# A new order of the first five attention units, and a last FFN group with the tokens on the partitions, both at once

## The chip, the cores and the metric

The kernel runs on one core of a Trainium2 chip. A core has five engines that run side by side, each taking its own instructions in order: TensorE (PE) multiplies matrices, VectorE (DVE), ScalarE (ACT) and GpSimd (POOL) work on elements, and SyncE (SP) here only issues DMAs. The metric is the device time of one execution in microseconds (us), the median over several executions.

## The reference

The program is one transformer layer in fp32: attention, then an FFN, each between two layer norms, with a residual added behind the second. x has 16 sequences of 256 tokens with 256 features.

```python
x = x + _layernorm(attn(_layernorm(x)))      # 16 heads of 128, causal softmax over 256 keys
x = x + _layernorm(ffn(_layernorm(x)))

# attn                                        # ffn; weights are 4-bit codes times a scale per block of 32
q = einsum('bpd,hde->bphe', x, W_Q) + b_Q     gate = einsum('th,nh->tn', xt, Wg)
k = einsum('bpd,hde->bphe', x, W_K) + b_K     up   = einsum('th,nh->tn', xt, Wu)
v = einsum('bpd,hde->bphe', x, W_V) + b_V     inter = gelu(gate) * up          # 2048 wide
z = softmax(causal(q k / sqrt(128))) v        out  = einsum('tn,hn->th', inter, Wd)
out = einsum('bqhe,hed->bqd', z, W_O) + b_O
```

## The kernel before

**Precision.** TensorE takes fp32r operands in one pass. To hold fp32 accuracy every large operand is split into a high half (the value rounded to fp32r, a copy on ACT) and a low half (the value less the high half, a subtraction on DVE or POOL), and a product is three matmuls, high by high, high by low, low by high (`mm3`). Small products (the own half of the scores, `qr` by `kr`) are true fp32 matmuls, which appear as two rows each. So each engine has its part in each operand: PE makes it, ACT the high half, DVE or POOL the low half.

**Attention.** The 4096 tokens are 8 blocks of 512 (two sequences). A unit is one head of one block, so there are 128 units; two heads make a pair, whose weights are split together. A unit passes these stages:

- `st_qk`: pk and pq, the keys and queries of 512 tokens, six matmuls of 512 columns each. ACT makes kh, kr, qh, qr; DVE makes kl, ql. pk and pq have one PSUM bank each, so the next unit's pk waits until ACT and DVE have read this one.
- `st_s`: scores of both sequences (sc), the mask and the row minimum on DVE (q carries a factor of -1/sqrt(128)), exp on ACT, the reciprocal rc on DVE, and the division pr on POOL.
- `st_t`, `st_w`, `st_b`: DVE transposes pr in 32x32 blocks (tr), four DMAs write it to HBM (hop) and one reads it back transposed (pt).
- `st_p`: high half of pt (ph) on ACT, low half (pl) on POOL.
- `st_v`: values of two pairs, one of four slices at a time (pv); `st_z`: z = v by probabilities (pz); `st_o`: the output projection, accumulated over the eight pairs (po).

The main loop runs over i from -5 to 129 and overlaps the stages: at step i it does the scores of unit i+4, q and k of unit i+5, pz of unit i, and between these it fills in other work by `slot`, which takes one piece from lists of pending jobs: weight splits (`splits`), layer norms (`urgent`, `behind`), the dequantization of FFN weights (`idle`). Of block 0 all raw weights come from HBM, are split and written back; later blocks load them already split. `w_split` is that split: high half on ACT, low half on POOL for v and o, on DVE for k and q.

**FFN.** It works on 1024 tokens at a time (superblocks of two blocks, bb = 0 and 1) in eight groups of 256 of the 2048 inner features, 32 groups in all. gate and up are made by a Strassen scheme with seven products in place of eight (m1 to m7), whose pieces ACT copies and DVE adds; gelu, the product and the halves of `inter` follow as a list of `pending` operations, of which one or two are issued beside each product. `st_d` multiplies the group before by wd and accumulates over the eight groups in four banks, pd (two blocks by two halves `dh` of the features). At a superblock's end `end` turns the sums so that the tokens lie on the partitions, and does layer norm and residual.

**The last group** has its own end, `st_last`: for four halves of 256 tokens (n = 0 to 3) it adds the last group's product, features on the partitions, to pd, copies it (oT on ACT), transposes it on PE (tpo, 16 transposes in all), takes mean and variance on DVE (one pow on POOL), and `apply` scales on DVE, shifts on ACT and sends it out: three outputs of 256 KB and two of 128 KB.

**Order.** Nothing is reordered by a scheduler: `run` (line 99 is where it calls every operation, so that all rows of the profile bear L99) ties each instruction behind the one issued before it on every engine, and `dma` (L88, L91) does that for SP. So the order in the source is the order on every engine, and an instruction that waits holds all behind it on its engine.

**The start.** While the first tokens are loaded, 30 transposes of the identity (`keep_warm`) run on PE; then `first_tokens` transposes the first normed tokens (tpx), and `w_split` makes the first weights.

Of the kernel before, what the change touches and what calls it, by code (L numbers as in the profile page):

```python
# [10 lines left out]
F32 = mybir.dt.float32  # L11
# [17 lines left out]
def kernel(  # L29
# [30 lines left out]
    def f(ap):  # L60
        return ap.bitcast(F32)
# [33 lines left out]
    def run(op, dst, *args, **kw):  # L95
        with ExitStack() as behind:
            for m in last.values():
                behind.enter_context(tc.issue_after(m))
            ins = op(dst, *args, **kw)  # L99
        last[ins.ins.engine] = ins.ins  # L100
        return ins
# [23 lines left out]
    def add(jobs, job, kind):  # L125
        jobs.append([job, 0, kind])
# [170 lines left out]
    def w_split(p, n):  # L297

        raw = RAW.pop((p, n)).rearrange("p (k c) -> p k c", k=2)
        key, done = p, True  # L300
        if n == "v":
            key, done = p // 2, p % 2
            w = HALF.pop(key) if done else w_tile(n)
            if not done:
                HALF[key] = w
            wv_ = w_view(w)[:, :, :, (p % 2) * 256 : (p % 2 + 1) * 256]
        else:
            w = w_tile(n)
            wv_ = w_view(w)
        c = qscale if n == "q" else 1.0  # L310
        run(nc.scalar.activation, wv_[:, 0], raw, AF.Copy, scale=c)
        if n in "vo" and (p, n) != (0, "v"):
            run(nc.gpsimd.tensor_tensor, wv_[:, 1], raw, f(wv_[:, 0]), ALU.subtract)
        else:
            run(nc.vector.scalar_tensor_tensor, wv_[:, 1], raw, c, f(wv_[:, 0]), ALU.mult, ALU.subtract)
        ahead = p + (2 if n == "v" else 1)
        if ahead < NG:
            w_raw(ahead, n)
        if done:
            W[key, n] = w_view(w)  # L320
            late.append((now[0] + 4, w_keep, (key, n, w)))
# [99 lines left out]
    def st_s(u):  # L421
        qh, ql, qr = Q.pop(u)
        kh, kl, kr = K.pop(u)
        pr = work.tile([P, 3, 2, P], F32, tag="pr", name="pr")
        mn = small.tile([P, 2, 2], F32, tag="mn", name="mn")
        sm = small.tile([P, 2, 2], F32, tag="sm", name="sm")
        rc = small.tile([P, 2, 2], F32, tag="rc", name="rc")
        parts = ((0, slice(0, 1)), (1, slice(1, 3)))
        scb = []
        for bi in range(2):  # L430
            sc = ps.tile([P, 3 * P], F32, tag="sc", name="sc", bufs=2)
            ks = slice(bi * S, (bi + 1) * S)
            run(nc.tensor.matmul, sc[:, 0:P], qr[:, bi, :], kr[:, bi, :], start=True, stop=True)
            mm3(sc[:, P:], [(lambda a: (qh, ql)[a][:, bi, :], lambda c: (kh, kl)[c][:, ks])])
            for q, cs in ((0, slice(0, P)), (1, slice(P, 3 * P))):
                run(
                    nc.vector.tensor_tensor_reduce,
                    sc[:, cs], sc[:, cs], mask[:, 2 * P - (cs.stop - cs.start) :], scale=1.0, scalar=3.0e38,
                    op0=ALU.add, op1=ALU.min, accum_out=mn[:, bi, q : q + 1],
                )  # L440
            scb.append(sc.rearrange("p (a c) -> p a c", a=3))
        while after:
            run(*after.popleft())
        for bi in range(2):
            for q, cs in parts:
                run(
                    nc.scalar.activation, pr[:, cs, bi, :], scb[bi][:, cs, :], AF.Exp,
                    bias=mn[:, bi, q : q + 1], scale=-1.0, accum_out=sm[:, bi, q : q + 1],
                )
            if bi:  # L450
                slot(V_, splits, idle, urgent, behind)
            run(nc.vector.reciprocal, rc[:, bi, :], sm[:, bi, :])
            for q, cs in parts:
                run(
                    nc.gpsimd.tensor_scalar, pr[:, cs, bi, :], pr[:, cs, bi, :], rc[:, bi, q : q + 1], 1.0,
                    ALU.mult, ALU.mult,
                )
        PR[u] = pr
# [22 lines left out]
    def st_p(u):  # L481
        pt = PT.pop(u).rearrange("p a m i -> p m a i")
        ph = work.tile([P, 2, 2, P], F32R, tag="ph", name="ph")
        pl = work.tile([P, 2, 2, P], F32R, tag="pl", name="pl")
        four = [t.rearrange("p c b (a i) -> p (c b) a i", a=4) for t in (ph, pl)]
        run(nc.scalar.copy, four[0], pt[:, 0:4])
        run(nc.gpsimd.tensor_tensor, four[1], pt[:, 0:4], f(four[0]), ALU.subtract)
        PH[u] = (ph, pl, pt)

    def st_z(u):  # L490
# [411 lines left out]
    def end(b, tr):  # L902
# [12 lines left out]
        for hf in range(2):  # L915
            dma(half(out, b, hf), X1[b][hf])

    def st_last():


        k = NGRP - 1
        while pending:
            run(*pending.popleft())
        w = FW[k, "d"]
        halves = [(bb, hf) for bb in (1, 0) for hf in range(2)]
        oTs, os, stats = {}, {}, {}

        def multiply(n, dh):
            bb, hf = halves[n]
            tok = slice(hf * S, (hf + 1) * S)  # L930
            cols = slice(dh * P, (dh + 1) * P)
            i = [quarter(k, c, bb) for c in range(2)]
            po = ACC[2 * NSB - 2 + bb, dh][:, tok]
            mm3(
                po, [(lambda a, c=c: w[:, a, c, cols], lambda s, c=c: i[c][:, s, tok]) for c in range(2)], MOVING_LAST,
                start=False, shared=True,
            )
            if dh == 0:
                oTs[n] = wide("oT").rearrange("p a b -> p (a b)")[:, 0 : 2 * S].rearrange("p (h n) -> p h n", h=2)
            run(nc.scalar.copy, oTs[n][:, dh], po)  # L940

        def turn_and_measure(n):
            tp = ps.tile([P, 2, D], F32, tag=("pk", "pq", "sc", "sc")[n], name="tpo", bufs=2 if n > 1 else 1)
            oT = oTs.pop(n)
            for t in range(2):
                for dh in range(2):
                    run(
                        nc.tensor.transpose,
                        tp[:, t, dh * P : (dh + 1) * P], oT[:, dh, t * P : (t + 1) * P], ident,
                    )  # L950
            os[n] = [tp[:, t, :] for t in range(2)]
            jobs = deque()
            stats[n] = None

            def measure():
                stats[n] = yield from ln_stats(os[n])

            add(jobs, measure(), V_)
            finish(jobs)

        def apply(n):
            bb, hf = halves[n]
            b = 2 * NSB - 2 + bb
            mv, rs = stats.pop(n)
            nb = ln_shift(mv, rs, 2)
            x1 = X1[b][hf]
            for t in range(2):
                run(
                    nc.vector.scalar_tensor_tensor,
                    x1[:, t, :], os[n][t], rs[:, t : t + 1], x1[:, t, :], ALU.mult, ALU.add,  # L970
                )
                run(nc.scalar.activation, x1[:, t, :], x1[:, t, :], AF.Identity, bias=nb[:, t : t + 1])
                if n == len(halves) - 1:
                    dma(half(out, b, hf)[:, t, :], x1[:, t, :])
            if n < len(halves) - 1:
                dma(half(out, b, hf), x1)

        count = len(halves)
        for n in range(count + 2):
            if n < count:  # L980
                multiply(n, 0)
            if 0 <= n - 1 < count:
                turn_and_measure(n - 1)
            if n < count:
                multiply(n, 1)
            if n >= 2:
                apply(n - 2)


    first = first_tokens()  # L990
# [13 lines left out]
        for n in range(count):  # L1004
            run(nc.tensor.transpose, warm[:, n % 4, :], ident, ident)

    keep_warm(30)
    add(urgent, first, V_)
    finish(urgent)
    run(nc.gpsimd.tensor_scalar, bqs, bqk[:, 0, :], qscale, 1.0, ALU.mult, ALU.mult)  # L1010
    for p in range(2):
        w_split(p, "v")
    for p, n in (2, "v"), (1, "k"), (1, "q"):
        w_get(p, n)

    def weights(*of):
        for pn, n in of:
# [3 lines left out]
    for i in range(-5, N + 2):  # L1021
        p = i // 2
        odd = i % 2 == 1
        if p >= 0 and not odd and p < len(pairs):
# [8 lines left out]
                    add(idle, f_make(*piece, pieces[m + 1] if m + 1 < len(pieces) else None), V_)  # L1033
            if b == NBLK - 1 and g == 0:
                add(spare, x_ops(0), N_)
        if 0 <= i + 4 < N:
            st_s(i + 4)
        slot(V_)
        if i + 5 < N:
            st_qk(i + 5)  # L1040
        slot(V_, urgent, behind)
        slot(G_)
# [19 lines left out]
            st_b(i + 3)  # L1062
        if 0 <= i + 4 < N:
            st_w(i + 4)
        if odd:
            weights((p + 1, "o"), (p + 5, "v"))
        else:
            weights((p + 4, "k"), (p + 4, "q"))
# [10 lines left out]
    for k in range(NGRP):  # L1079
# [18 lines left out]
        slot(V_)  # L1098
        slot(A_ + G_)
        st_d(k - 1, 1, 1)  # L1100
        slot(V_)
        slot(A_ + G_)
        if k > 0:
            parts(k, "m7", "m3")
        if k == NGRP - 1:
            parts(k, "m4")
        st_d(k - 1, 0, 0)
        slot(V_)
        slot(A_ + G_)
# [4 lines left out]
        slot(A_ + G_)  # L1114
    finish(urgent)
    finish(behind)
    st_last()


# [49 lines left out]
```

## Time and profile before

| | us |
|---|---|
| median of 3 runs | 1517.89 (1517.84 to 1518.86) |
| profiled execution | 1517.91, its span 1516.1 |
| PE busy | 1498.9 (99%) |
| DVE busy | 1185.8 (78%) |
| ACT busy | 1037.0 (68%) |
| POOL busy | 728.9 (48%) |
| first pk to first pz | 9.24 to 43.84 |
| last pe matmul, last tpo group, last output issued | 1496.87, 1508.61, 1513.2 |

Times inside the profile count from the start of the span; the execution's own time has 1.8 us more around it. The granted clock of TensorE is 0.998 over the span. A row of the timeline gives the start, the length, the engine, the operation and how many of them run together; in square brackets stands the idle time of the engine ahead of it and what ended that. Lengths of matmuls contain the way through the array, so the step from one start to the next is what one costs. The list of waits names what PE waited for: sum in us, how often, the longest.

### The profile page before, as it was taken

The page shows a single profiled execution, that of the slowest core. Times are in us where ns is not written, and L with a number is a line of the kernel's source. Part 1 is how long each engine was busy: PE and PEld are TensorE (multiplying, and loading weights), DVE is VectorE, ACT ScalarE, POOL GpSimd, SP SyncE. Part 2 cuts the span into 40 slices and gives each one's busy share as a digit, 9 for nine tenths or more (in the row PEclk, how much of TensorE's full clock was granted, in tenths as well). Part 3 has the DMA queues.
Part 4 walks back from the last instruction along what each step waited for, and adds up shares of the span by engine and source line. Part 5 has one row for each costly group of instructions (what it writes and reads, how often), then busy time and mean ns, then how long its engine had stood idle before and what let it go on. Part 6 is the DMA issues. An engine that isn't in the chain of part 4 may idle for free.

```text
span 1516.1 us, 25754 instructions
## 1 busy us (share of the span) xinstructions
PE 1498.9 (99%) x7831; PEld 1278.7 (84%) x7831; DVE 1185.8 (78%) x3011; ACT 1037.0 (68%) x2614; POOL 728.9 (48%) x951
## 2 busy tenths in 40 slices
PE   8999999999999999999999999999999999999997
PEld 7888888888888888888888888887888888888886
DVE  6876787787787888788778787777887887787866
ACT  6877766777677677676677767676766665666565
POOL 3755578677667776866876876880000000000000
PEclk9999999999999999999999999999999999999999
DMA  8998899999899999899899999977557465655561
GB/s 292 339 319 264 262 305 312 286 306 312 281 294 326 282 315 310 274 318 305 274 285 314 306 296 320 316 239 272 210 193 262 182 248 196 250 180 198 219 233 58
DMA packets 200426, 407.55 MB, mean 269 GB/s; under 512 B 21472, under 2 KB 128480, under 8 KB 189536
## 3 DMA queue, kind: packets, MB, share of 16 engines
q1 hardware_dynamic: 200288, 405.91, 79.9%
q8 instruction: 62, 1.02, 0.3%
q14 instruction: 76, 0.62, 0.1%
HBM read 294.15 MB, written 111.67 MB: 268 GB/s over the span
## 4 chain that ended last, share of the span: by engine, by line
PE 94%; DVE 2%; ACT 1%; DMA 1%; POOL 1%; issue 1%; SPq 0%; POOLq 0%; DVEq 0%; ACTq 0%
PE pd L99 13%; PE pk L99 11%; PE pv L99 11%; PE pq L99 11%; PE po L99 11%; PE pz L99 10%; PE sc L99 9%; PE pa L99 8%; PE pf L99 5%; PE pe L99 2%; DVE sum L99 1%; DMA rawq<-in_wq 0%; DMA rawv<-in_wv 0%; ACT pr L99 0%; DVE inter L99 0%
## 5 line engine op out<-in xcount | busy, mean ns | idle before, releaser
L99 POOL TENSOR_SCALAR pr<-pr,rc 128x128 f32<-128x128 f32 (+1 forms) x512 | 250.1, 504 | 90.7 <-DVE rc L99 90.7
L99 ACT ACTIVATE pr<-sc,mn 128x128 f32<-128x128 f32 (+1 forms) x512 | 208.2, 419 | 87.5 <-DVE mn L99 87.5
L99 POOL TENSOR_TENSOR rs<-rs,mhalf 128x4 f32<-128x4 f32 (+1 forms) x35 | 34.5, 985 | 485.1 <-DVE rs L99 275.0
L99 POOL TENSOR_TENSOR pl<-pt,ph 128x512 fp32r<-128x512 f32 x128 | 165.0, 1289 | 190.0 <-ACT ph L99 178.0
L99 DVE CUSTOM_DVE_ANT_0 sc<-sc,mask 128x128 f32<-128x128 f32 (+1 forms) x512 | 180.8, 374 | 67.8 <-PE sc L99 59.1
L99 PE MATMUL pv<-wv,xT 128*128 128x512 f32 x768 | 208.9, 407 | 0.0
L99 ACT ACTIVATE zh<-pz,bqk 128x512 fp32r<-128x512 f32 x128 | 88.3, 690 | 167.7 <-PE pz L99 167.6
L99 PE MATMUL pk<-xT,wk 128*128 128x512 f32 x768 | 199.5, 395 | 0.3 <-POOL xT L99 0.2
L99 PE MATMUL pd<-inter,wd 128*128 128x512 f32 (+1 forms) x792 | 197.8, 385 | 1.4 <-ACT inter L99 1.0
L99 PE MATMUL pq<-xT,wq 128*128 128x512 f32 x768 | 196.3, 391 | 0.0
L99 PEld LDWEIGHTS pd<-inter,wd 128*128 128x128 f32 x792 | 144.9, 188 | 34.5 <-DVE inter L99 2.9
L99 PEld LDWEIGHTS pq<-xT,wq 128*128 128x128 f32 x768 | 144.2, 188 | 32.9
L99 ACT COPY part<-pa 128x512 f32<-128x512 f32 x192 | 111.6, 585 | 68.0 <-PE pa L99 65.5
L99 PE MATMUL po<-zh,wo 128*128 128x512 f32 x512 | 157.7, 389 | 0.0
L99 PEld LDWEIGHTS pk<-xT,wk 128*128 128x128 f32 x768 | 134.9, 188 | 23.8 <-POOL xT L99 0.7
L99 PEld LDWEIGHTS pv<-wv,xT 128*128 128x128 f32 x768 | 135.0, 189 | 23.6
L99 DVE SCALAR_TENSOR_TENSOR zl<-pz,bqk,zh 128x512 fp32r<-128x512 f32 x128 | 95.9, 749 | 74.0 <-ACT zh L99 73.9
L99 ACT CAST inter<-sum 128x512 fp32r<-128x512 f32 x128 | 80.1, 626 | 87.5 <-DVE sum L99 87.5
L99 DVE TENSOR_TENSOR inter<-sum,inter 128x512 fp32r<-128x512 f32 x128 | 89.0, 695 | 56.9 <-ACT inter L99 55.9
L99 DVE STREAM_TRANSPOSE tr<-pr 128x768 f32<-128x768 f32 x128 | 123.3, 963 | 1.7 <-DMA hop<-tr 1.2
L99 DVE SCALAR_TENSOR_TENSOR kl<-pk,bqk,kh 128x512 fp32r<-128x512 f32 x128 | 96.1, 751 | 30.7 <-ACT kr L99 26.9
L99 PEld LDWEIGHTS po<-zh,wo 128*128 128x128 f32 x512 | 96.0, 188 | 19.9
(149 smaller groups left out, 3723.0 us busy)
## 6 DMA issues: line engine op xcount, KB each, us to landing
hop<-tr SPq DMA_DIRECT2D x512, 96.0 KB
pt<-hop SPq DMA_DIRECT2D x128, 384.0 KB
wk<-wk SPq DMA_DIRECT2D x64, 512.0 KB
wq<-wq SPq DMA_DIRECT2D x64, 512.0 KB
wo<-wo SPq DMA_DIRECT2D x64, 512.0 KB
wu<-fu SPq DMA_DIRECT2D x32, 1024.0 KB
wg<-fg SPq DMA_DIRECT2D x32, 1024.0 KB
wv<-wv SPq DMA_DIRECT2D x56, 512.0 KB
```

What stands on the lines that cost most here:

```text
L99: ins = op(dst, *args, **kw)
```

## The change

Five parts, made together:

1. `keep_warm` runs 27 transposes instead of 30.
2. In the first five steps (i < 0) `st_qk(i + 5)` is issued ahead of `st_s(i + 4)` instead of behind it, two slots for weight splits follow the scores, the slot for splits inside the softmax is left out for units below 4, and the split of v of pair 2 is asked for at i = -4 instead of ahead of the loop.
3. The low halves of the k and q weights of pairs 1 to 3 are made by POOL instead of DVE. For q, whose factor the DVE instruction applied on the way, POOL first multiplies the raw weights in place.
4. The low half of the probabilities, pl, of the last four units is made by DVE instead of POOL.
5. In the last group the sums of the first seven groups are copied by ACT (`copy_last`) and multiplied by the identity in true fp32 (`base_last`, eight matmuls of 128x128 for each block), which lays them with the tokens on the partitions into fresh banks; the last group's product is then made in that form too, with the tokens stationary and wd moving (48 matmuls of 256 columns as before), and added there. The 16 transposes and the eight copies oT of 256 columns fall away. `apply` scales and shifts on ACT for n < 3, and adds the residual on POOL, or, for the second tile of n = 0 and 1, on DVE after all multiplies were issued; the outputs are eight of 128 KB.

```diff
-        if n in "vo" and (p, n) != (0, "v"):
+        if n in "vo" and (p, n) != (0, "v") or n in "kq" and 1 <= p <= 3:
+            if n == "q":
+                run(nc.gpsimd.tensor_scalar, raw, raw, c, 1.0, ALU.mult, ALU.mult)
             run(nc.gpsimd.tensor_tensor, wv_[:, 1], raw, f(wv_[:, 0]), ALU.subtract)
...
-            if bi:
+            if bi and u >= 4:
                 slot(V_, splits, idle, urgent, behind)
...
-        run(nc.gpsimd.tensor_tensor, four[1], pt[:, 0:4], f(four[0]), ALU.subtract)
+        engine = nc.vector if u >= N - 4 else nc.gpsimd
+        run(engine.tensor_tensor, four[1], pt[:, 0:4], f(four[0]), ALU.subtract)
...
+    def copy_last(bb):
+        OT[bb] = wide("oT").rearrange("p a b -> p (a b)").rearrange("p (h n) -> p h n", h=2)
+        for dh in range(2):
+            run(nc.scalar.copy, OT[bb][:, dh], ACC.pop((LAST[bb], dh)))
+
+    def base_last(bb):
+        oT = OT.pop(bb)
+        for hf in range(2):
+            to = BASE[bb, hf] = ps.tile([P, 2, D], F32, tag=(("po0", "po1"), ("pv", "pz"))[bb][hf], name="base")
+            for t in range(2):
+                for dh in range(2):
+                    run(
+                        nc.tensor.matmul, to[:, t, dh * P : (dh + 1) * P],
+                        oT[:, dh, (2 * hf + t) * P : (2 * hf + t + 1) * P], ident,
+                        start=t == 0 and dh == 0, stop=False, skip_group_check=True,
+                    )
...
+        def multiply(n):
             bb, hf = halves[n]
             i = [quarter(k, c, bb) for c in range(2)]
             for t in range(2):
+                tok = slice((2 * hf + t) * P, (2 * hf + t + 1) * P)
+                mm3(
+                    BASE[bb, hf][:, t, :],
+                    [(lambda s, c=c: i[c][:, s, tok], lambda a, c=c: w[:, a, c, :]) for c in range(2)],
+                    start=False, shared=True,
+                )
...
+            if n < 3:
+                fa = wide("fa")
+                for t in range(2):
+                    ln_apply_act(fa[:, t, :], o[t], nb, rs, t)
+                    where = nc.vector if t and n < 2 else nc.gpsimd
+                    todo = (where.tensor_tensor, x1[:, t, :], x1[:, t, :], fa[:, t, :], ALU.add)
+                    if where is nc.vector:
+                        rest.append((todo, to[:, t, :], x1[:, t, :]))
+                    else:
+                        run(*todo)
+                        dma(to[:, t, :], x1[:, t, :])
...
+        for n in range(4):
+            multiply(n)
+            if n == 1:
+                base_last(0)
+            measure(n)
+            if n:
+                apply(n - 1)
+        for todo, to, x1 in rest:
+            run(*todo)
+            dma(to, x1)
+        apply(3)
...
-    keep_warm(30)
+    keep_warm(27)
...
-    for p, n in (2, "v"), (1, "k"), (1, "q"):
-        w_get(p, n)
+    for n in "kq":
+        w_get(1, n)
...
+        if i < 0:
+            while after:
+                run(*after.popleft())
+            st_qk(i + 5)
         if 0 <= i + 4 < N:
             st_s(i + 4)
+        if i < 0:
+            for _ in range(2):
+                slot(V_, splits)
         slot(V_)
-        if i + 5 < N:
+        if 5 <= i + 5 < N:
             st_qk(i + 5)
...
+        if i == -4:
+            w_get(2, "v")
...
         st_d(k - 1, 1, 1)
+        if k == NGRP - 1:
+            copy_last(1)
...
             parts(k, "m4")
+            base_last(1)
         st_d(k - 1, 0, 0)
...
     finish(behind)
+    copy_last(0)
     st_last()
```

More of the change, by code (lines that the diff above doesn't have):

```diff
@@ L916, in end @@
             dma(half(out, b, hf), X1[b][hf])
+    OT = {}
+    BASE = {}
+    LAST = [2 * NSB - 2, 2 * NSB - 1]
+    def copy_last(bb):
[13 more added lines that the diff above has]
+                    )
     def st_last():
@@ L925, in st_last, with measure, work_ @@
         halves = [(bb, hf) for bb in (1, 0) for hf in range(2)]
-        oTs, os, stats = {}, {}, {}
-        def multiply(n, dh):
+        stats, sums = {}, {}
+        rest = []
+        def multiply(n):
             bb, hf = halves[n]
-            tok = slice(hf * S, (hf + 1) * S)
-            cols = slice(dh * P, (dh + 1) * P)
             i = [quarter(k, c, bb) for c in range(2)]
[L933 to L944, printed above, removed]
-            for t in range(2):
[L946 to L951, printed above, removed]
-            jobs = deque()
[L953 to L958, printed above, removed]
+            for t in range(2):
+                tok = slice((2 * hf + t) * P, (2 * hf + t + 1) * P)
[4 more added lines that the diff above has]
+                )
+        def measure(n):
+            jobs = deque()
+            o = [BASE[halves[n]][:, t, :] for t in range(2)]
+            def work_():
+                mv, rs = yield from ln_stats(o)
+                stats[n] = o, mv, rs
+            add(jobs, work_(), V_)
             finish(jobs)
@@ L962, in apply @@
             bb, hf = halves[n]
-            b = 2 * NSB - 2 + bb
-            mv, rs = stats.pop(n)
+            o, mv, rs = stats.pop(n)
             nb = ln_shift(mv, rs, 2)
[L966 to L987, printed above, removed]
+            x1 = X1[LAST[bb]][hf]
+            to = half(out, LAST[bb], hf)
+            if n < 3:
[9 more added lines that the diff above has]
+                        dma(to[:, t, :], x1[:, t, :])
+            else:
+                for t in range(2):
+                    run(
+                        nc.vector.scalar_tensor_tensor,
+                        x1[:, t, :], o[t], rs[:, t : t + 1], x1[:, t, :], ALU.mult, ALU.add,
+                    )
+                    run(nc.scalar.activation, x1[:, t, :], x1[:, t, :], AF.Identity, bias=nb[:, t : t + 1])
+                    dma(to[:, t, :], x1[:, t, :])
+        for n in range(4):
[9 more added lines that the diff above has]
+        apply(3)
     first = first_tokens()
```

## The prediction

> **What bounds the kernel now.** I read the page's busy shares first, then the list of all waits of PE, then three stretches of the timeline: the start, the seam between attention and FFN, and the tail.
>
> ```profile
> PE 1498.9 (99%) x7831; PEld 1278.7 (84%) x7831; DVE 1185.8 (78%) x3011; ACT 1037.0 (68%) x2614; POOL 728.9 (48%) x951
> ```
> PE works 99% of the span, so the change can save or lose only where PE waits, or where it adds or removes PE work, or behind PE's last matmul.
>
> ```profile
> PE sc L99 <- ACT qr L99: 5.1, 4, 2.0
> PE warm L99 <- POOL ident masks.py:199: 1.6, 1, 1.6
> PE pd L99 <- ACT inter L99: 1.0, 3, 0.4
> PE pz L99 <- POOL pl L99: 0.9, 1, 0.9
> ...
> PE tpo L99 <- ACT oT L99: 0.3, 1, 0.3
> ```
> These are PE's waits (sum in us, times, longest). Nearly all of the 5.1 us lies in the first five units; the `pl` wait is one, at the seam.
>
> ```profile
> 9.24 1.62 PE L99 MATMUL pk<-xT,wk 128*128 128x512 f32 x6
> ...
> 20.81 0.49 PE L99 MATMUL sc<-kr,qr 128*128 128x128 f32 x2 [1.96 <-ACT qr L99]
> ...
> 43.84 0.28 PE L99 MATMUL pz<-ph,vh 128*128 128x256 f32 x1
> ```
> From the first matmul to the first pz: 34.6 us. By the same timeline pk+pq take 2.73 (41.12 to 43.84), a unit's scores 1.32 (20.81 to 22.13), a pv 1.40: 6x2.73 + 5x1.32 + 4x1.40 = 28.6, so 6.0 us are stalls.
>
> ```profile
> 36.52 0.83 POOL L99 TENSOR_SCALAR pr<-pr,rc 128x128 f32<-128x128 f32 x2 [3.84 <-DVE rc L99]
> 38.52 1.11 POOL L99 TENSOR_SCALAR pr<-pr,rc 128x128 f32<-128x128 f32 x2 [1.17 <-DVE rc L99]
> 40.33 1.29 POOL L99 TENSOR_TENSOR pl<-pt,ph 128x512 fp32r<-128x512 f32 x1 [0.70 <-DMA hop<-tr]
> 41.58 1.29 POOL L99 TENSOR_TENSOR wo<-rawo,wo 128x512 fp32r<-128x512 f32 x1
> 43.21 1.62 POOL L99 TENSOR_SCALAR pr<-pr,rc 128x128 f32<-128x128 f32 x4 [0.34 <-DVE rc L99]
> ```
> POOL before pz(0): `pl` is finished at 41.6, 2.5 us before PE uses it at 44.07, and nothing but pr stands ahead of it.
>
> ```profile
> 1499.46 0.62 ACT L99 CAST inter<-sum 128x512 fp32r<-128x512 f32 x1 [1.43 <-DVE sum L99]
> 1500.86 2.51 PE L99 MATMUL pd<-inter,wd 128*128 128x256 f32 x16 [0.22 <-DVE inter L99]
> ...
> 1503.20 0.60 PE L99 MATMUL tpo<-ident,oT 128*128 128x128 f32 x4
> ...
> 1508.32 5.28 SPq L91 DMA_DIRECT2D out<-xs  x5
> ```
> The tail: the cast of the last group's `inter` opens the final multiplies; the last of five output DMAs is issued at 1513.2.
>
> **The change part by part.** The sum is made against the profiled execution: 1517.91 us, span 1516.1 and 1.8 around it; that is the median of 1517.89. For start and tail I walked each engine's new order forward, every instruction starting when its engine is free and its inputs done, with the durations of before's rows.
>
> *Start, fewer warm transposes and the new order.* Three warm transposes less at 0.11 (3 in 7.58 to 7.91): -0.3, because the token transposes (7.15) follow the last warm one directly. In the new order PE has pk/pq(1) in front of sc(0), and pv+pk/pq in front of each later score, so qr has more cover. The stalls left in the walk: 0.7 at pk(1) (its bank is free only after kr(0) on ACT), 0.9 at one pv, 2.2 before sc(4), where only pv lies between sc(3) and it; together 3.9 instead of 6.0. First pz at 41.6 instead of 43.84: **-2.3**. The lo halves of pairs 1 and 2 on POOL fall into its idle time (3.84 before 36.52); the moved (2,v) fetch and the earlier weight DMAs on SP shift no operand that PE waits for, since the raws land before their splits. If they did not, a k/q DMA would show as a wait of ACT for wk, priced among the rivals.
>
> *Start, lo halves of k,q of pair 3 on POOL.* They are issued ahead of `pl` of unit 0. In the walk POOL ends pr(3) at 39.3 and then runs wk lo 1.25, raw*c, wq lo 1.26, pl 1.25. The price of raw*c (one 128x512 tensor_scalar) is not in the trace. Near rows: pr, the same operation with one scalar, 0.48 for 128 and 0.52 for 256 columns on average, alone 0.83 for the two; xn with two pointer scalars 1.23 for 256 columns. Bounds 0.52 and 2x1.23=2.46; I take 0.70, since pr is the same kind and 0.83 buys 384 columns with two starts. pl is then done at 43.8, while PE wants it at 41.8: a **new stall of 2.0**. Queued behind it on POOL are wo lo (1.29) and pr(4) (1.63), which ends at 46.7 instead of 44.8; pr(4) holds tr (0.97), zl (0.75) and the masks of unit 5 on DVE, these hold exp(5) on ACT, and that the copies up to qr(6): sc(6) waits 1.2 instead of 0.1, **+1.1**. Net of the start -2.3+2.0+1.1 = **+0.8**; each us more of raw*c goes on 1:1, so from +0.6 to +3.0 (the walk with 2.46 gave +3.5, because the next unit slips too).
>
> The Trainium skill speaks against this move: "GPSIMD Engine Reference", section "Engine selection", sends elementwise work to the Vector engine because two-input operations take about twice as long on GpSimd. The rows agree in size (1.29 against 0.69), but the rule by itself would price it at 4x0.6=2.4, while here the queue makes it 3.1. The page's "Elementwise" section has 768 ns for a one-input loop of 512 elements; with that estimate for raw*c the start would be +0.9.
>
> *Seam.* `pl` of the last four units goes from POOL (1.29) to DVE (0.69).
>
> ```profile
> 1006.62 2.45 POOL L99 TENSOR_SCALAR xn<-xs,mv,rs 128x256 f32<-128x256 f32 x2
> 1009.04 1.26 POOL L99 TENSOR_TENSOR pl<-pt,ph 128x512 fp32r<-128x512 f32 x1
> ...
> 1010.36 0.39 PE L99 MATMUL pz<-pl,vh 128*128 128x256 f32 x1 [0.88 <-POOL pl L99]
> ```
> POOL has xn ahead of pl; DVE is busy 4.3 of the 8 us from 1004 to 1012, so it does pl well before 1009.5: **-0.9**. Bounds 0 and -0.9.
>
> *Tail.* T is the start of the last pe matmul (1496.87). Before pd's twelve matmuls there now stand eight fp32 matmuls of base_last(1). Their price: from 44.19 (pt,vr, the same fp32 128x128) to 44.54 lie one such and one 256-column matmul, 0.35-0.12=0.23; 8 of them 1.8. Nothing covers them, PE being the bound there. pd ends at T+4.7 instead of T+2.9. ACT runs in order, and copy_last(0) puts two copies of pd ahead of the waiting cast: the second starts when pd is done, 0.48 later the cast starts, at T+5.4 instead of T+2.6 (1499.46). Cast to the first final multiply and lo half on DVE as before: the multiplies flow from T+6.8 instead of T+4.0: **+2.8**. From there before ran 48 multiplies, 16 transposes and 2 waits to 1509.43 = T+12.6; now 46x0.118 and the second base_last 1.8 end at T+14.2, so **PE ends 1.65 later**, the transposes (16x0.09) and their waits being gone.
>
> The Trainium skill's "FP8 and Floating Point Precision", "TensorE Precision Notes", gives true FP32 four passes: 4x128 columns cost what 512 do, 1.8 for eight by the 0.23 of such a step. The rows of tpo (0.36 for four, 1503.20 to 1503.56), to which a multiplication by the identity looks alike, would give 0.7 a base_last, and the tail 1.8 to 2.2 less.
>
> copy_last(1) costs ACT two copies of 0.48 in the last group, where it had 1.91 idle ahead of the cast at 1496.88; I cost it at nothing (without that cover 1.0).
>
> Behind PE: statistics, pow and POOL's two adds for n=2, then SP, which now issues eight outputs of 128 KB instead of five, takes n=2's two, the two deferred ones and the last two, in that order. An add of 256 columns on POOL lies between 0.46 (128 columns, 64 rows `full<-full`) and 1.29 (512); I take 0.73, in proportion. In the walk n=2's second output is issued at T+17.7 and four more issues follow 0.39 and 3x0.48 apart: the last at T+19.55, instead of T+16.29 (1513.16). The landing (1.9 before) stays. Tail **+3.3**; with the adds at their bounds +2.8 to +5.0, contention of the deferred DVE adds with POOL up to +0.4.
>
> Sum: +0.8 - 0.9 + 3.3 = +3.2, with a little for that contention: 1517.9+3.3 = **1521.2**.
>
> **The rivals.**
> 1. *The start keeps its gain.* If POOL is through pair 3's halves before about 40.5 (2 us earlier than in the walk), pz(0) does not wait and pr(4) is not late: 1517.9-2.3-0.9+3.3 = 1518.0. For it: POOL's gap of 3.84 before 36.52. Against: its queue is in order, and pr(3) waits for exp(3), which sits ahead of the halves.
> 2. *POOL is dearer.* raw*c at 2.46 and the tail's adds at 1.29: +2.7+1.7 on 1521.2 = 1525.6; one of them alone 1523 to 1524. For it: xn's 1.23. Against: pr's 0.52.
> 3. *Faster.* The start loses all its stalls, 6.0+0.3, and no new one comes: 1517.9-6.3-0.9+3.3 = 1514.0. It decides if ACT, DVE and POOL each keep under PE's 5.45 a unit (2.73+1.32+1.40) with nothing queued between exp and the next qr. Against: DVE alone is busy 25.2 of the 35 us from 9 to 44, and masks, exp, pr, tr stand in one chain.
> 4. *The identity is cheap.* base_last as the transposes: 1519.2.
>
> **How the numbers follow.** A measurement of this kernel tells about 0.2% (3.0 us) from no change: 1514.9 and 1520.9. Chances: forecast 0.52 (its own range 1520.3 to 1522.6, longer upwards by the contention), rival 1 0.16, rival 2 0.19, rival 3 0.06, rival 4 0.07. Slower is rival 2 and three quarters of the forecast: 0.58; faster rival 3: 0.06; within: 0.36. The range leaves out rival 3, the lower part of rival 1 and the upper half of rival 2: 1518.2 to 1523.9.
>
> **What would show it.** Start: the first pz about 2 us earlier, PE waiting for `pl` there and for qr at sc(6). Seam: no pz wait for POOL. Tail: two oT copies ahead of the `inter` cast on ACT, base matmuls 0.22 apart, the last output issued 19.5 after the last pe matmul. It is wrong if pz(0) finds pl ready, if raw*c takes over 1 us, or if base matmuls step by 0.11.

## The result, and the profile after

The changed kernel takes 1522.89 us (median of eight), the kernel before 1518.94 in the same comparison: 3.95 us more, a ratio of 1.0024 with a 95% interval from 1.0016 to 1.0033. The prediction was 1521.2 from 1517.9, that is +3.3, in a range of 1518.2 to 1523.9. The direction, the size and the places were right. Of the three terms of the sum, the seam was off by 0.3 us, the tail by 0.6 and the start, by execution, by 0.1 to 1.1, and one thing happened that no step had named. Of the 1.7 us by which the time itself was missed, 1.0 is the base: the kernel before took 1517.89 in the runs that the prediction started from and 1518.94 here.

The profiled execution has a span of 1521.4. The busy line of its page:

```profile
PE 1502.3 (99%) x7844; PEld 1282.0 (84%) x7844; DVE 1183.0 (78%) x3005; ACT 1038.1 (68%) x2610; POOL 736.3 (48%) x960
```

PE has 3.4 us more busy time; part of it is the slower clock shown below. The list of PE's waits of the changed kernel (sum in us, how often, the longest):

```profile
PE sc L99 <- ACT pr L99: 2.1, 1, 2.1
...
PE base L99 <- ACT inter L99: 1.2, 1, 1.2
PE pv L99 <- DVE vl L99: 1.1, 2, 0.8
...
PE sc L99 <- ACT qr L99: 0.8, 1, 0.8
PE pk L99 <- DVE kl L99: 0.6, 1, 0.6
PE pz L99 <- POOL pl L99: 0.6, 1, 0.6
```

The 5.1 us of waits for qr are down to 0.8, and four other waits have taken their place: for exp ahead of sc(4) (2.1), for vl, for kl, and for pl at the first pz. The wait of 0.9 at the seam is gone. Its rows in the timeline, DVE starting pl 1.1 us before PE takes it:

```profile
1009.92 0.75 DVE L99 TENSOR_TENSOR pl<-pt,ph 128x512 fp32r<-128x512 f32 x1
...
1011.03 0.28 PE L99 MATMUL pz<-pl,vh 128*128 128x256 f32 x1
```

The start, PE's rows of the timeline of the changed kernel:

```profile
9.53 1.60 PE L99 MATMUL pk<-xT,wk 128*128 128x512 f32 x6
...
38.19 0.80 PE L99 MATMUL sc<-kr,qr 128*128 128x128 f32 x2 [2.15 <-ACT pr L99]
...
43.74 0.28 PE L99 MATMUL pz<-ph,vh 128*128 128x256 f32 x1
...
44.69 0.39 PE L99 MATMUL pz<-pl,vh 128*128 128x256 f32 x1 [0.55 <-POOL pl L99]
...
59.92 0.28 PE L99 MATMUL pz<-ph,vh 128*128 128x256 f32 x1
```

The first pz comes at 43.74 as before (43.84), not at 41.6, and the third, from which on up to the seam every unit takes the same time in both kernels, 1.7 later (58.21 before). The queue on POOL that the prediction had named is there, row for row, about 0.8 later than in its walk:

```profile
38.43 1.63 POOL L99 TENSOR_SCALAR pr<-pr,rc 128x128 f32<-128x128 f32 x4 [4.13 <-DVE rc L99]
40.02 1.29 POOL L99 TENSOR_TENSOR wk<-rawk,wk 128x512 fp32r<-128x512 f32 x1
41.40 0.62 POOL L99 TENSOR_SCALAR rawq<-rawq 128x512 f32<-128x512 f32 x1
42.10 1.29 POOL L99 TENSOR_TENSOR wq<-rawq,wq 128x512 fp32r<-128x512 f32 x1
43.36 1.28 POOL L99 TENSOR_TENSOR pl<-pt,ph 128x512 fp32r<-128x512 f32 x1
```

But PE came late to it, because of something else. In the windows of the changed kernel (stretch, length, busy time and instructions of PE, PEld, DVE, ACT and POOL, granted clock, DMA share, GB/s) the granted clock falls to half for 3.4 us, right behind the wait ahead of sc(4):

```profile
34.80:38.20 3.40, 1.25 (x7) 0.69 (x5) 3.06 (x12) 1.51 (x7) 0.00 (x0) 1.00 1.01 313
38.20:41.60 3.40, 3.40 (x13) 3.21 (x14) 1.77 (x6) 3.30 (x9) 3.08 (x6) 0.50 0.98 374
41.60:45.00 3.40, 2.85 (x14) 2.25 (x14) 1.68 (x9) 3.07 (x12) 3.32 (x4) 1.00 0.98 335
```

The tail, rows of the timeline of the changed kernel:

```profile
1498.61 1.95 PE L99 MATMUL base<-ident,oT 128*128 128x128 f32 x16
...
1503.34 0.59 ACT L99 COPY oT<-pd 128x512 f32<-128x512 f32 x1 [0.77 <-PE pd L99]
1503.82 0.62 ACT L99 CAST inter<-sum 128x512 fp32r<-128x512 f32 x1
...
1505.22 2.90 PE L99 MATMUL base<-wd,inter 128*128 128x256 f32 x22 [0.22 <-DVE inter L99]
...
1510.94 8.04 SPq L91 DMA_DIRECT2D out<-xs  x8
```

Counted from the start of the last pe matmul (T, here 1498.38), the cast stands at T+5.4 and the flow of multiplies at T+6.8, both as predicted. PE ends at T+14.4 (14.2 predicted) and the last output is issued at T+20.20 (19.55 predicted, 16.29 before).

### The profile page after: what moved, and what is told of

Same layout as the page of the kernel before. It is cut to its first block, busy times and chain, and to the rows that moved or that the text cites. A ratio compares the mean times of both kernels' runs of the same rounds, so it can differ in the third digit from the quotient of the medians.

```text
span 1521.4 us, 25795 instructions
## 1 busy us (share of the span) xinstructions
PE 1502.3 (99%) x7844; PEld 1282.0 (84%) x7844; DVE 1183.0 (78%) x3005; ACT 1038.1 (68%) x2610; POOL 736.3 (48%) x960
## 4 chain that ended last, share of the span: by engine, by line
PE 93%; DVE 2%; ACT 2%; POOL 1%; issue 1%; DMA 1%; SPq 0%; POOLq 0%; DVEq 0%; ACTq 0%
PE pd L99 13%; PE pk L99 11%; PE pv L99 11%; PE pq L99 11%; PE po L99 11%; PE pz L99 9%; PE sc L99 9%; PE pa L99 8%; PE pf L99 5%; PE pe L99 3%; DVE sum L99 1%; PE base L99 1%; DMA wu<-fu 1%; PE warm L99 0%; ACT pr L99 0%
## 5 line engine op out<-in xcount | busy, mean ns | idle before, releaser
L99 POOL TENSOR_TENSOR pl<-pt,ph 128x512 fp32r<-128x512 f32 x124 | 160.0, 1291 | 184.8 <-ACT ph L99 175.4
L99 PE MATMUL pd<-inter,wd 128*128 128x512 f32 x744 | 190.7, 391 | 1.0 <-ACT inter L99 1.0
L99 PEld LDWEIGHTS pd<-inter,wd 128*128 128x128 f32 x744 | 138.8, 188 | 33.2 <-DVE inter L99 2.4
L99 PEld LDWEIGHTS pv<-wv,xT 128*128 128x128 f32 x768 | 134.7, 189 | 24.9 <-DVE vl L99 1.5
```

## The experiments

Two ways to explain the start stood against each other: F, POOL's queue ahead of pl, as predicted; and C, the half clock. For the tail: ACT's order and the outputs behind PE (F, O), or the fp32 matmuls themselves (B). All of them compute the whole layer.

The times of e1 to e6 and e9 against before have intervals of some 1.4 us to either side, and e7 and e8 were timed in one execution each, so single profiles, read row by row, carry most of what follows. The table has the eleven profiles, in us from the start of the span; "clock up" is where the steps of the first matmuls fall from 0.21 to 0.11, "half clock" a stretch at half the granted clock between 10 us and the end of PE's work.

| kernel | clock up | first pk | first pz | third pz | third pz less first pk | half clock | T to last output issued |
|---|---|---|---|---|---|---|---|
| before | 6.3 | 9.24 | 43.84 | 58.21 | 48.97 | - | 16.29 |
| e2 (start as before) | 4.4 | 8.67 | 43.74 | 58.14 | 49.47 | 21.4-24.9 | 20.18 |
| e9 (start as before) | 5.9 | 8.77 | 43.91 | 58.28 | 49.51 | - | 16.30 |
| changed | 7.5 | 9.53 | 43.74 | 59.92 | 50.39 | 38.2-41.6 | 20.20 |
| e1 | 7.6 | 9.61 | 43.91 | 60.01 | 50.40 | 38.3-41.7 | 16.29 |
| e3 | 5.9 | 8.74 | 41.64 | 59.08 | 50.34 | - | 18.24 |
| e7 | 5.9 | 9.06 | 42.00 | 59.43 | 50.37 | - | 16.27 |
| e5 | 7.0 | 9.28 | 42.18 | 60.15 | 50.87 | 44.5-47.9 | 16.91 |
| e4 | 5.7 | 8.90 | 41.81 | 58.52 | 49.62 | - | 20.21 |
| e6 | 5.4 | 8.74 | 41.69 | 58.39 | 49.65 | - | 16.28 |
| e8 | 5.7 | 8.73 | 39.76 | 59.06 | 50.33 | 1050.1-1053.5 | 16.29 |

### e1: all but the last group

The changed kernel with `st_last` of before, and without the calls

```diff
-            copy_last(1)
...
-            base_last(1)
...
-    copy_last(0)
```

> The change without its part 5: the last group as before, with 16 transposes. Theory F, the forecast: start +0.8, seam -0.9, so -0.1 us against before (within 1 us), and all of the loss of the whole change is in the last group. Rival C: the start alone already costs 1.5 us or more, because TensorE runs at half its clock for three microseconds after the wait ahead of sc(4) (granted clock 0.50 from 38.2 to 41.5 in the profile of the changed kernel): +1 to +2 against before. If the slow stretch is an accident of one execution, this profile shows none and PE waits about 2 us for pl at the first pz.

Measured: ratio 1.0008 (0.9999 to 1.0017), +1.2 us; the forecast's -0.1 is just inside. The half clock appears again, at the same place, and the third pz is 1.8 later than in before, so up to here C stands as well as F. T to the last output is 16.29, to the hundredth as in before: whatever the new tail costs is in part 5 alone.

### e2: the last group alone

The kernel before with `st_last` of the changed kernel, and the calls

```diff
+            copy_last(1)
...
+            base_last(1)
...
+    copy_last(0)
```

> Before with part 5 alone. Theory F: +3.3 us, with the last pe matmul where it was, the last multiply 1.6 later and the last output issued 3.3 to 3.8 later relative to the last pe matmul. Rival: the new tail is worth nothing by itself and the loss of the whole change comes from the start: within 1 us of before.

Measured: 1.0028 (1.0019 to 1.0037), +4.2 us, T to the last output 20.18. So the tail is worth +3.9 by the profiles, and the rival is out. This profile had a surprise: the start of before loses its clock too, as its windows show, behind its own longest wait, the one ahead of sc(1):

```profile
18.00:21.40 3.40, 1.15 (x8) 0.84 (x7) 2.94 (x6) 2.98 (x7) 1.48 (x3) 1.00 0.68 192
21.40:24.80 3.40, 3.40 (x13) 2.81 (x12) 2.60 (x11) 2.08 (x9) 0.63 (x2) 0.51 0.92 267
```

### e3: the cast ahead of the copies

In the changed kernel:

```diff
         while pending:
             run(*pending.popleft())
+        copy_last(0)
...
     finish(behind)
-    copy_last(0)
     st_last()
```

> The changed kernel, with the copies of the first block's sums (copy_last(0)) issued behind the pending operations of the last group instead of ahead of them. Theory F (ACT's order holds the cast): the cast starts 2.6 instead of 5.4 after the last pe matmul, multiplies 2.0 earlier (they then wait for pd, which the eight fp32 matmuls still delay), the end 1.8 earlier than the changed kernel, about +2 against before. Rival B (the 16 fp32 matmuls of 0.22 are what costs, wherever the cast stands): no more than 0.5 earlier than the changed kernel.

Measured: 1.0021 (1.0012 to 1.0030), +3.2 us; its profile holds 2.0 us of waits for a weight DMA (wu) in the FFN, which the changed kernel's list does not have, so the rows decide. Tail of e3, with T at 1499.71:

```profile
1502.29 0.62 ACT L99 CAST inter<-sum 128x512 fp32r<-128x512 f32 x1 [1.43 <-DVE sum L99]
...
1504.46 3.04 PE L99 MATMUL base<-wd,inter 128*128 128x256 f32 x24
...
1510.31 8.04 SPq L91 DMA_DIRECT2D out<-xs  x8
```

The cast is at T+2.6, the multiplies flow from T+4.75, PE ends at T+12.45, where before ended at T+12.56, and the last output is issued at T+18.24: **1.96 of the tail's 3.9 us were ACT's order**. And rival B falls: with ACT's order mended, the 16 fp32 matmuls (0.22 each in the steps of PE's rows, two rows of 0.11) cost no more than the transposes, oT copies and waits that they replace.

This execution kept its clock, and there the start is the predicted one: first pz at 41.64, and

```profile
43.86 0.39 PE L99 MATMUL pz<-pl,vh 128*128 128x256 f32 x1 [1.82 <-POOL pl L99]
```

a wait of 1.8 for pl (2.0 predicted), the third pz 0.87 later than in before (0.8 predicted). That this is so close is in part luck: the first pk came at 8.74 here, 0.2 ahead of the 8.94 that the prediction had.

### e4: pair 3 on DVE

In the changed kernel:

```diff
-        if n in "vo" and (p, n) != (0, "v") or n in "kq" and 1 <= p <= 3:
+        if n in "vo" and (p, n) != (0, "v") or n in "kq" and 1 <= p <= 2:
```

> The changed kernel with the low halves of k and q of pair 3 on DVE, as before. Theory F (POOL's queue ahead of pl makes the loss of the start): pl is ready when PE comes, no wait at the first pz, and 1.1 us or more come off the changed kernel. Rival C (the half clock after the wait ahead of sc(4) sets when the first pz starts): the wait for pl goes, but the first pz still starts at 43.5 or later and no more than 0.6 us come off.

Measured: 1.0027 (1.0017 to 1.0037), +4.1 us, which can't be told from the changed kernel. In the profile the wait for pl is gone and the third pz stands 49.62 behind the first pk instead of 50.34 to 50.40 (changed, e1, e3, e7): 0.75 comes off, not the 1.1 of F. The rest has turned into a wait for qr at the next scores:

```profile
45.76 0.49 PE L99 MATMUL sc<-kr,qr 128*128 128x128 f32 x2 [1.24 <-ACT qr L99]
```

This execution kept its clock, so rival C was not tried by it; e7 does that.

### e5: the outputs earlier

In the kernel of e3:

```diff
-            if n < 3:
+            if n < 2:
...
             measure(n)
+            if n == 3:
+                for todo, to, x1 in rest:
+                    run(*todo)
+                    dma(to, x1)
             if n:
                 apply(n - 1)
-        for todo, to, x1 in rest:
-            run(*todo)
-            dma(to, x1)
         apply(3)
```

> The kernel of e3 (copies behind the pending operations) with the third half (n=2) scaled on DVE and shifted on ACT as the fourth is, so without its two adds on POOL, and with the two deferred outputs issued ahead of those of n=2. Theory O (what is left of the tail's loss lies behind PE, in POOL's adds and in the order of SP's issues): the last output is issued 16.7 to 17.2 after the last pe matmul, where e3 has 18.2 and before 16.3, and the end is 1.1 to 1.5 earlier than e3. Rival B (the fp32 matmuls): PE ends as in e3 at 12.4 after the last pe matmul and the last output stays at 18.

Measured: 1.0009 (1.0000 to 1.0018), +1.4 us. PE ends at T+12.46 as in e3, the last output is issued at T+16.91: **1.33 more of the tail's loss were POOL's two adds and the order of SP's issues** (the two were changed together), and 0.6 is left. The two rows that matter in e5, seven outputs in one run on SP while POOL does nothing but the last pow:

```profile
1513.49 3.49 SPq L91 DMA_DIRECT2D out<-xs  x7
1513.63 0.75 POOL L99 TENSOR_TENSOR rs<-rs,mhalf 128x2 f32<-128x2 f32 x1 [0.17 <-DVE rs L99]
```

### e7: filling the wait ahead of sc(4)

In the kernel of e1:

```diff
+        if i == 0:
+            keep_warm(10)
         if 0 <= i + 4 < N:
             st_s(i + 4)
```

> The kernel of e1 with the ten transposes alone, pair 3 on POOL. Clock theory: full clock throughout from 10 us on, first pz at 41.6, then a wait of 1.8 to 2.0 for pl, and the third pz 0.9 later than in before, as in e3; in e1 the half clock took the place of most of that wait and left the third pz 1.8 later. Rival: the half clock comes from something else than PE's idle time and appears again at 38.

One execution, 1518.54 us. The ten transposes bring the wait down from 2.2 to 1.06, the granted clock is 1.00 from 10 us to the end of PE's work, first pz at 42.00, and the wait for pl is 1.8 again:

```profile
44.21 0.39 PE L99 MATMUL pz<-pl,vh 128*128 128x256 f32 x1 [1.82 <-POOL pl L99]
```

The third pz stands 50.37 behind the first pk, against 50.39 and 50.40 in the two executions that lost their clock at 38; e3, the same start without the transposes and with its clock, has 50.34. So **rival C falls** for the changed kernel and e1: counted from the first pk, the half clock makes PE 1.3 us later at the first pz (34.21 against 32.94), a place where it would have waited for pl by that much anyway. It is not free everywhere: in e5, whose start is the same, the clock fell at 44.5, behind the wait for pl, and there the third pz stands 50.87 behind the first pk, 0.5 more than in the others, and the wait for qr ahead of sc(6), 0.8 in them, is taken up by it. The expectation had it wrong that e1's third pz was late because of the clock; it was late because its first pk was (9.61 against 9.06).

### e8: the new order for one more unit

In the kernel of e1, with pair 3 on DVE as in e4:

```diff
-        if i < 0:
+        if i < 1:
             while after:
                 run(*after.popleft())
             st_qk(i + 5)
...
-        if 5 <= i + 5 < N:
+        if 1 <= i and i + 5 < N:
             st_qk(i + 5)
```

> The kernel of e1 with pair 3 on DVE and the new order carried on by one unit: q and k of unit 5 are issued ahead of sc(4), so that the 2.2 us in front of sc(4) are filled with work. If the stalls of PE in the start were what the start costs, the third pz would come 2 us earlier than in e4. Theory L (the chain behind PE, from exp over pr and tr to the next masks, sets the pace, and PE's order only moves the stalls): first pz at 39.7, 2 us earlier still, and yet the third pz no earlier than in e4 and up to 1.2 later.

One execution, 1522.85 us, and as theory L said: first pz at 39.76, two more us gained, and the third pz at 59.06, no earlier than in e4, relative to the first pk 0.7 later. PE's rows in e8:

```profile
39.76 0.39 PE L99 MATMUL pz<-ph,vh 128*128 128x256 f32 x1 [0.36 <-ACT ph L99]
...
41.56 0.38 PE L99 MATMUL pz<-pl,vh 128*128 128x256 f32 x1 [1.30 <-POOL pl L99]
...
53.66 0.49 PE L99 MATMUL sc<-kr,qr 128*128 128x128 f32 x2 [1.55 <-ACT qr L99]
```

The 2.2 us wait ahead of sc(4) is gone, and the time comes back at ph (0.4), at pl (1.3) and at the scores of units 5 (0.6) and 6 (1.6). The long time of this execution comes from elsewhere: from its first to its last pe matmul it takes 472.7 us (468.0 to 468.6 in the executions that do not wait for wu), of which 2.5 are waits for wu, and behind the longest of these, 2.04 us, the clock fell to half:

```profile
1046.69:1050.10 3.41, 1.37 (x6) 0.85 (x6) 2.05 (x5) 1.10 (x2) 0.00 (x0) 1.00 0.78 286
1050.10:1053.51 3.41, 3.41 (x9) 2.66 (x9) 1.37 (x3) 1.17 (x3) 0.00 (x0) 0.50 1.03 420
```

### e6 and e9: candidates

e6 is the kernel of e1 with pair 3 on DVE as in e4 and the ten transposes of e7. e9 is the kernel before with

```diff
-        run(nc.gpsimd.tensor_tensor, four[1], pt[:, 0:4], f(four[0]), ALU.subtract)
+        engine = nc.vector if u >= N - 4 else nc.gpsimd
+        run(engine.tensor_tensor, four[1], pt[:, 0:4], f(four[0]), ALU.subtract)
...
-    keep_warm(30)
+    keep_warm(27)
...
+        if i == -3:
+            keep_warm(10)
```

> Candidate: the kernel of e1 (last group as before) with pair 3's low halves back on DVE and ten transposes of the identity ahead of sc(4), where PE waits 2.2 us. Clock theory: no window of 3.4 us has over 1.4 us of idle PE, so the granted clock stays 1.0 from 10 us on in every execution; the first pz is at 41.7 (shifted with the first pk), and against before the start gives -0.3 and the seam -0.6: -0.5 to -1 us, more on executions in which before loses its clock. Rival: the transposes delay the scores or the clock drops all the same: no gain against e1 (+1.2).

> Candidate: the kernel before with its own start and its own last group, pl of the last four units on DVE, 27 warm transposes and ten transposes of the identity ahead of sc(1), where PE of before waits 2.2 us. Theory: the seam gives -0.6 (0.96 at the pz and 0.36 given back), the warm transposes nothing by the third pz because the waits for qr take them up, and the clock stays at 1.0 from 10 us on: 0.6 us faster than before, 1 where before loses its clock; below what the times can tell apart, so that the profile has to show it: no wait of pz for pl at the seam, first pe 0.6 earlier against the third pz.

Measured: 0.9998 (0.9989 to 1.0007) and 0.9999 (0.9990 to 1.0007). Neither can be told from before. In both profiles the clock stays up from 10 us on. e6's third pz is 0.2 later than before's, its first pe 0.4 earlier. e9's third pz is where before's is, with a first pk 0.5 earlier; its first pe is 0.5 earlier; then it waits 1.6 for wu. So no version tried beats before by an amount that can be measured.

## Why the prediction was right, point by point

- **The start, forecast +0.8; measured +0.9 to +1.9 in five profiles of this start (changed, e1, e3, e5, e7; third pz against 58.21).** The steps were right: the waits for qr go, pl is held up by pair 3's halves, raw*c took 0.62 (0.70 taken), the wait for pl is 1.8 (2.0 taken), and the first pz at 41.64 in e3 is the forecast's 41.6. The three stalls of the walk, 0.7, 0.9 and 2.2 (3.8 in sum, not 3.9), measured 0.6, 1.1 and 2.1. At sc(6) the wait was 0.8, not 1.2. What was mis-sized is the first term: the walk carried the first pk along with the three transposes saved, 0.3 ahead of before's 9.24. In the runs the first pk lies between 8.67 and 9.61, with the moment at which the clock comes up, and the third pz of the new start follows it (50.34 to 50.40 behind it in changed, e1, e3, e7; the forecast's own terms give 48.97+0.3+0.8 = 50.07), while that of before does not (58.14 to 58.28 for first pks of 8.67 to 9.24). The 4x0.6 that the prediction sets beside its own price counts four low halves where pair 3 has two, 2x(1.29-0.69) = 1.2; no term of its sum rests on it.
- **The step that no part of the prediction had**: the half clock from 38.2 to 41.6. It put the first pz to 43.74 and shrank the wait for pl to 0.55, so two of the signs named in advance ("first pz about 2 us earlier", "PE waiting for pl there") looked half wrong in the profile of the changed kernel, although the third pz was not touched (e3, e7).
- **The seam, forecast -0.9; measured -0.6.** The wait of 0.9 is gone in all profiles with pl on DVE: from pz 60 to the start of the last pz the time falls by 0.96. But 0.36 comes back from there to the first pe: 7.00 to 7.03 us (changed, e1, e3, e4) against 6.65 (before, e2). The bound 0 to -0.9 held it. The rows place the 0.36 within the last pz itself: from its last matmul to the first pe both kernels take 5.6, and from its first row to its last the changed kernel takes 1.42, before 1.05. In the changed kernel PE starts the last pz at 1023.01, its next matmul at 1023.21 and the one with pl only 0.31 later (0.12 in before), just behind the end of pl on DVE (1023.46), which had made zl first. So some 0.2 of the 0.36 is a wait for pl on its new engine, as these rows read; no run tried it. The rows of pl and of PE in the changed kernel:

```profile
1022.78 0.68 DVE L99 TENSOR_TENSOR pl<-pt,ph 128x512 fp32r<-128x512 f32 x1
...
1023.52 0.39 PE L99 MATMUL pz<-pl,vh 128*128 128x256 f32 x1
```

The same matmul in before:

```profile
1022.49 0.28 PE L99 MATMUL pz<-pl,vh 128*128 128x256 f32 x1
```

- **The tail, forecast +3.3; measured +3.9** (20.18 to 20.21 against 16.29, three profiles). The cast behind the oT copies was right to 0.1. Too small were: PE's end by 0.2, the final multiplies stepping by 0.120 instead of 0.118 and the first one behind the second base_last by 0.20; and the way from there, by 0.4, where the forecast had named contention "up to 0.4". The rows show some 0.3 of it, all of it beside the deferred adds on DVE: the last pow on POOL takes 0.82 instead of 0.70, and POOL then stands idle 0.15 for ACT's scaling of n=2 (fa). For n=0 and 1 that starts 0.04 behind the end of nb, here 0.42 behind it (nb ends at 1514.20), and its row puts the wait down to the first of the deferred adds (xs); why was not tried. POOL's add of 256 columns, interpolated at 0.73, was 0.73.

```profile
1514.29 0.82 POOL L99 TENSOR_TENSOR rs<-rs,mhalf 128x2 f32<-128x2 f32 x1 [0.17 <-DVE nb L99]
...
1514.62 1.02 ACT L99 ACTIVATE fa<-base,nb,rs 128x256 f32<-128x256 f32 x2 [0.93 <-DVE xs L99]
...
1515.26 1.41 POOL L99 TENSOR_TENSOR xs<-xs,fa 128x256 f32<-128x256 f32 x2 [0.15 <-ACT fa L99]
```

- **The rivals.** Rival 1 (the start keeps its gain) did not occur: POOL is through pair 3's halves at 43.4, not 40.5. Rival 2's dear prices did not either. Rival 3, the faster one, named as the point of decision that nothing be queued between exp and the next qr; e8 shows for one more unit why it did not come: filling PE's waits moves them to where the chain of masks, exp, pr and tr ends next. Rival 4 fails by the measured 0.22 a matmul by the identity (0.23 taken).

The terms of the single profiles add up to +0.9 to +1.9, -0.6 and +3.9: 4.2 to 5.2 us, most of it inside the interval of the measured ratio (2.4 to 5.0 us). All three came out worse than forecast, so the total of the medians (+3.95 against +3.3) was met more closely than the sum of the parts, and that much of it is luck.

## What to carry to other kernels

Before PE's order is changed to fill its waits, look at whether the chain behind it can go faster: in a pipeline that is being filled, PE's first result 2 us (or, in e8, 4 us) earlier bought nothing at the third, and the place to measure is where the steady state begins. Where engines run strictly in order, a copy that frees something early must not stand ahead of the operation that the end hangs on; moving one call by a few lines (e3) was worth half of the tail's loss. Work that is handed to an idle engine holds up what stands in its queue behind it: pair 3's halves on POOL held pl, and PE by 1.8 us at the first pz; giving them back (e4) was worth 0.75 at the third.

## What the runs showed of the hardware

The granted clock of TensorE is given out in windows of 3.4 us that run on by themselves, and a wait much shorter than a window can cost the next one half of its speed. In the eleven profiles the clock came up between 4.4 and 7.6 us, though the first matmul starts at 1.6 in all of them. Where it fell again, it did so at a multiple of 3.41 us behind that moment, for one such length: in the changed kernel 7.5 + 9x3.41 = 38.2, in e2 4.4 + 5x3.41 = 21.4, in e5 7.0 + 11x3.41 = 44.5. In e8 it fell in the FFN, at 1050.1, which is 306 times 3.413 behind 5.6. Cut into these windows, PE had by its rows been idle for 2.15 (changed), 2.16 (e1), 2.25 (e2), 1.88 (e5) and 2.04 us (e8) in the window before; windows with up to 1.7 us idle (1.67 in e3's FFN, from 1046.9) were never followed by a drop, and of two windows with 1.9 in e5 one was. The same 2.2 us wait that fell across two windows (1.35 and 0.81 in e3) did not bring the clock down. So one wait of 2 us costs in some executions of a kernel and not in others, by when the clock came up.

The Trainium skill's "TensorE: Matmul & The Clock Gate", "What's actually happening", has the free-running window of 3413 ns, which these rows agree with; its advice in "Why this matters for your kernels", no idle gaps over about 3 us, is not strict enough by them.

The weight DMA of the FFN's second group is the other thing that differs between executions of the same code: in seven of the eleven profiles PE does not wait for it, in four it waits 1.1 (e5) to 2.5 us (e8). In three of the four (e3, e8, e9) SP, in whose order the weight DMAs stand, issues the read of ohop ahead of them 4.1 to 4.3 us behind the last of four writes, in the other eight profiles 2.4 to 2.8; the 1.1 of e5 is not explained by that. The wait is as much as most of the terms above, and it is why times alone could not separate them.
